# Two-layer graph network on one core: finished rows placed late, incoming rows on ScalarE, gates by row, adjacency streamed

## The chip, the cores and the metric

One core of a Trainium2 chip runs the whole kernel. A core has five engines, each with its own instruction stream that is executed in order: TensorE (PE: matmuls and transpositions), VectorE (DVE), ScalarE (ACT), GpSimd (POOL) and SyncE (SP), which here issues every DMA. [...] an instruction that waits holds up everything behind it on its engine. The metric is the device time of one launch in microseconds (us); less is better.

## The reference

Inputs: x of 16 batches, 1024 rows, 256 channels; a 1024x1024 adjacency; everything in float32.

```python
# layer 0
A_hat = (adj + I) scaled by deg**-0.5 on both sides
agg   = einsum('nm,bmd->bnd', A_hat, x)
h     = relu(batchnorm(agg @ W1.T))          # 512 wide, moments over all 16*1024 rows
y     = batchnorm(h @ W2.T)                  # 256 wide, likewise
x     = layernorm(x + y)
# layer 1, for each batch
c     = mean of x over channels              # one number per row
A     = |abs(sigmoid(c_m - c_n) - 0.5) - 0.5| * 2
g     = relu((x.T @ (adj * A)) * para)       # queries, q = g.T
k, v  = split(x @ kv_w)
attn  = softmax(q k.T * scale) over 1024 rows, 4 heads of 64
x     = layernorm(x + attn v)
```

## The kernel before

**Layer 0.** The adjacency is normalised and transposed, and aggregation and the two linear layers run over all batches, with block products arranged in a scheme of seven (`seven`). The second batch normalisation needs all rows, so its result y lies in DRAM and is normalised when it is fetched again. In this phase, `load_weights` also fetches what layer 1 keeps: `kvw`, `para_sb` and the whole adjacency `adj_sb` (32 KB of each partition).

**Layer 1** is a software pipeline over 16 batches, written out by hand. A batch has `NS` = 16 attention steps; a step is one half of the query columns (`hf`), one pair of heads and a quarter of the key rows. For a step g, `scores` makes the logits in PSUM on PE (two buffers), `exps` the exponentials on ACT (`e`, six buffers, two a step), `sums` adds them on DVE into the running denominators `acc`, and `attend` multiplies by the values on PE. All other work is cut into pieces that are placed in slots: `put(w, t, f, ...)` puts a piece into slot t of batch w. A batch has `NC` = 8 slots; slots beyond 7 belong to the next batch. Two slots make one turn, so that a batch has four turns, called 0 to 3 here. A turn issues first all pieces of its two slots and then its four attention steps. While batch b runs through attention, the slots hold:

- for batch b+1: the eight gate rows (`gate`, three in slot 0, three in slot 1, two in slot 2), keys, values (slots 0 to 2), and the query matmuls (`graph`, slots 2 to 7, with `queries` on DVE as each of four groups ends);
- for batch b+2: `load` of y and x blocks, four blocks of 256 rows (slots 0 to 3), `bn2_q` on POOL (slots 1 to 4), `rows` (transposition and residual on DVE) and `ln1_a` (statistics on DVE, inverse root on POOL) in slots 2 to 5, `ln1_b` (the normalisation itself, with a sum per row for the mean c) in slots 3 to 6, `put_x1`, `get_x1` and `x1_v` (a transposed copy by way of DRAM), `means`, and `crow` (the means as a row, broadcast by DMA);
- for batch b and the one before: `dens` (denominators by a matmul with ones, copied by ACT to `dt`), `recips`, `fetch_o` (attention output back from DRAM), `finish_a` (transposition, division, residual and statistics on DVE, scale and shift on POOL), `finish_b` (normalisation on ACT and the output DMA).

The order inside a slot is made by `arrange`: `dens` first, then `bn2_q`, then the long PE pieces (`keys`, `values`, `graph`) with the others between them by `rank`, gates ahead of them or spread among them, `recips` before the second long piece, `crow` last. In slots with `graph` the gates go first.

A gate row i is `wg_a` on ACT and, two gates later, `wg_b` on DVE. Two forms compute the same: even rows take Abs and then Tanh on ACT (lines 698, 699), odd rows a Tanh of the signed difference (line 696), whose sign bit DVE then sets with an OR (line 705). Line 706 then multiplies by the adjacency row block (128x1024).

In batch 0 there is an opening of its own (`ln1_a0`, `ln1_b0`, `gate0`, `graph0`): its rows are normalised on ACT, and PE does its query matmuls while batch 1's blocks come in. Batch 1's transposed copy is made by PE (`x1_t`). The last batch has no batch behind it.

Layer 1 assumes that no exponential overflows; it counts bad denominators, and `general`, which runs only if there are any, computes a batch again. It doesn't run with these inputs.

Of the kernel before, what the change touches and what calls it, by code (L numbers as in the profile page):

```python
# [16 lines left out]
P = 128  # L17
# [5 lines left out]
def gnn_norm_attention_kernel(  # L23
# [66 lines left out]
    c_dram = [dram.tile([NT, P], F32, name=f"crow_d{b}") for b in range(B)]  # L90
    LDP = 2
# [32 lines left out]
    with ExitStack() as l0:  # L124
# [282 lines left out]
        adj_sb = keep.tile([P, NT, N], F32, name="adj_sb")  # L407
        yts, xrs = {}, {}

        def load_weights(k):  # L410

            if k == 1:
                nc.sync.dma_start(kvw, kv_w.rearrange("(c p) f -> p c f", p=P))
            if 1 <= k <= NT // 2:
                i = 2 * (k - 1)
                nc.sync.dma_start(
                    adj_sb[:, i : i + 2, :], adj[i * P : (i + 2) * P, :].rearrange("(c p) m -> p c m", p=P)
                )
            if k == NT // 2 + 1:
                nc.sync.dma_start(para_sb, para.rearrange("o (c p) h w -> p c (o h w)", p=P))  # L420
# [139 lines left out]
    def fast():  # L560
      with ExitStack() as fx:
        pool = lambda name, bufs, **k: fx.enter_context(tc.tile_pool(name=name, bufs=bufs, **k))
        x1p = pool("x1p", 11)
# [8 lines left out]
        sm = pool("sm", 5)  # L572
        rp = pool("rp", 2)
# [40 lines left out]
        def ln1_a(b, j):  # L614
# [7 lines left out]
            mvs[b, j] = ln_stats(sm, x1s[b, j], f"a{b}_{j}")  # L622

        def ln1_b(b, j):
            mv, rs = mvs.pop((b, j))
            for a in range(2):
                r = x1s[b, j][:, a, :]
                nc.vector.scalar_tensor_tensor(
                    r,
                    r,  # L630
                    mv[:, a, 0:1],
                    rs[:, a : a + 1].to_broadcast([P, C]),
                    op0=OP.subtract,
                    op1=OP.mult,
                    accum_out=css[b][:, 2 * j + a : 2 * j + a + 1],
# [54 lines left out]

        def wg_a(b, i):
            t = wgp.tile([P, N], F32, tag="wg", name=f"wg_{b}_{i}")
            wgs[b, i] = t
            if i % 2:
# [6 lines left out]
        def wg_b(b, i):  # L701
            t = wgs[b, i]
            if i % 2:
                ti = t.bitcast(mybir.dt.int32)
                nc.vector.tensor_scalar(ti, ti, -(2**31), None, op0=OP.bitwise_or)
            nc.vector.scalar_tensor_tensor(t, t, 1.0, adj_sb[:, i, :], op0=OP.add, op1=OP.mult)  # L706
# [147 lines left out]
        def fetch_o(b, j):  # L854
# [3 lines left out]
            t = OB[b, j] = otp.tile([P, 2, C], F32, tag="ob", bufs=1, name=f"ob{b}_{j}")  # L858
# [83 lines left out]
        for b in range(B):  # L942

            for hf in range(NH):
# [3 lines left out]
                for k in range(KB // 2):  # L948
                    put(b, t + k, fetch_o, b, hf * (KB // 2) + k)
                    put(b, t + 1 + k, finish_a, b, hf * (KB // 2) + k)  # L950
                    late = 0 if b == B - 1 else 1
                    if b == B - 1 and hf == 0:
                        late = NC - t - 2 - k
                    put(b, t + 2 + k + late, finish_b, b, hf * (KB // 2) + k)
# [60 lines left out]
        def arrange(pieces):  # L1015
            first = [fa for fa in pieces if fa[0] is dens]
# [3 lines left out]
            alone = [fa for fa in pieces if fa[0] in (recips, crow)]  # L1020
# [20 lines left out]
            k = ([n for n, fa in enumerate(order) if fa[0] in long] + [len(order)] * 2)[1]  # L1041
            order[k:k] = [fa for fa in alone if fa[0] is recips]
# [4 lines left out]

        nm0 = {}

        def ln1_a0(j):  # L1050
            ln1_a(0, j)
            mv, rs = mvs.pop((0, j))
            nm = sm.tile([P, 2], F32, tag="nm", name=f"nm_a{j}")
            for a in range(2):
                nc.gpsimd.tensor_scalar(
                    nm[:, a : a + 1], mv[:, a, 0:1], rs[:, a : a + 1], -1.0, op0=OP.mult, op1=OP.mult
                )
            nm0[j] = nm, rs

        def ln1_b0(j):  # L1060
            nm, rs = nm0.pop(j)
            for a in range(2):
                r = x1s[0, j][:, a, :]
                i = 2 * j + a
                nc.scalar.activation(
                    r, r, AF.Identity, bias=nm[:, a : a + 1], scale=rs[:, a : a + 1], accum_out=css[0][:, i : i + 1]
                )
# [243 lines left out]
```

## Time and profile before

| | |
|---|---|
| time, median of 3 runs (lowest, highest) | 2517.84 us (2513.79, 2518.4) |
| the profiled execution, its time | 2517.56 us |
| its span in the profile | 2515.8 us |
| mean granted TensorE clock | 0.993 |
| from the start to the second linear layer's first stall | 610 us |
| layer 1's opening, up to the first score matmul | about 810 to 876 us |
| one batch in attention | 103.7 to 104.2 us |
| HBM traffic | 225.71 MB, 89 GB/s over the span |

The profile gives busy time by engine; groups of instructions by source line; waits, as "engine tile line <- what ended the wait: us in total, times, longest us"; and a timeline, whose columns are start, duration, engine, line, operation, output<-inputs, shapes and count, and in brackets the idle time ahead of it with what ended it. A tile's name stands without its number: `s` are the logits, `e` the exponentials, `acc` the running denominators, `pd` and `dt` the denominators, `wg` the gate rows, `pg` the query matmuls, `pk` and `pv` keys and values, `o` and `ot` the attention output, `ob` the same fetched back, `r` the finished rows, `yt` and `xr` incoming blocks, `nm` and `rs` a block's shift and scale.

### The profile page before, as it was taken

The numbers are of one execution on the slowest core, as the hardware profiler recorded it, in microseconds if no ns is written. First come the engines' busy times: TensorE is split into PE (matmuls) and PEld (weight loads), VectorE is DVE, ScalarE is ACT, GpSimd is POOL, SyncE is SP. The second block draws the span as 40 slices with busy tenths as digits, with TensorE's granted clock in tenths as the row PEclk, the third lists the DMA queues.
The fourth block names the chain that finished last, engine by engine and source line by source line (L and its number), as shares of the span: only waits on it lengthen the run. The fifth ranks groups of instructions, "written<-read, shape, count | busy, mean of one in ns | idle before, by whom it ended". The sixth has DMA issues, their size and how long they took to land.

```text
span 2515.8 us, 33531 instructions
## 1 busy us (share of the span) xinstructions
PE 2437.9 (97%) x12341; PEld 1024.0 (41%) x12341; DVE 1847.9 (73%) x2776; ACT 1037.3 (41%) x1325; POOL 694.2 (28%) x706
## 2 busy tenths in 40 slices
PE   8999999998999899999999999999999999999997
PEld 4444444443444443443434434334334343343432
DVE  5545554556767777887878879788797887978667
ACT  2000000003453355464564645636456365563644
POOL 2232322232565222222322213222132231322112
PEclk9999999999999999999999999999999999999998
DMA  3122212221796223333333333333333334333111
GB/s 134 67 84 101 99 68 84 100 97 58 265 324 201 43 55 81 68 77 80 80 76 73 77 79 77 76 79 76 80 75 74 79 73 90 71 68 89 27 42 44
DMA packets 545770, 225.71 MB, mean 90 GB/s; under 512 B 388680, under 2 KB 533696, under 8 KB 538432
## 3 DMA queue, kind: packets, MB, share of 16 engines
q1 hardware_dynamic: 545600, 223.50, 33.4%
q8 instruction: 99, 1.62, 0.3%
q14 instruction: 71, 0.58, 0.1%
HBM read 129.52 MB, written 93.91 MB: 89 GB/s over the span
## 4 chain that ended last, share of the span: by engine, by line
PE 49%; DVE 15%; ACT 7%; issue 2%; DMA 1%; SPq 0%; DVEq 0%; POOL 0%; ACTq 0%; POOLq 0%
PE pg L746 13%; PE s L772 13%; PE o L808 12%; PE po L483 7%; DVE acc L793 5%; DVE wg L706 2%; ACT wg L696 2%; ACT wg L698 1%; PE pv L732 1%; PE pd L835 1%; ACT wg L699 1%; ACT kT L724 1%; DVE st_a L551 1%; ACT e L784 1%; DVE x L607 1%
## 5 line engine op out<-in xcount | busy, mean ns | idle before, releaser
L784 ACT ACTIVATE e<-s 128x1024 f32<-128x1024 f32 x512 | 496.4, 1021 | 547.1 <-PE s L772 483.5
L793 DVE TENSOR_TENSOR acc<-acc,e 128x1024 f32<-128x1024 f32 x384 | 507.2, 1321 | 83.3 <-ACT e L784 54.0
L772 PE MATMUL s<-qT,kT 64*64 64x512 f32 x4096 | 491.8, 595 | 27.7 <-ACT e L784 26.9
L808 PE MATMUL o<-e,v 64*64 64x512 f32 x4096 | 486.1, 589 | 0.0
L746 PE MATMUL pg<-wg,x 128*128 128x512 f32 x960 | 424.9, 595 | 0.0
L603 POOL TENSOR_TENSOR yt<-yt,stq 128x512 f32<-128x512 f32 x120 | 181.3, 1511 | 446.9 <-DMA yt<-yT 185.3
L772 PEld LDWEIGHTS s<-qT,kT 64*64 64x64 f32 x4096 | 147.6, 133 | 320.2 <-issue 263.3
L808 PEld LDWEIGHTS o<-e,v 64*64 64x64 f32 x4096 | 157.0, 133 | 284.0 <-issue 271.4
L746 PEld LDWEIGHTS pg<-wg,x 128*128 128x128 f32 x960 | 178.7, 190 | 226.4 <-issue 218.7
L66 POOL TENSOR_SCALAR rs_z<-mv_z 128x2 f32<-128x2 f32 x64 | 28.2, 441 | 662.9 <-DVE mv_z L552 653.3
L102 ACT COPY u<-pa 128x512 f32<-128x512 f32 x15 | 8.8, 585 | 475.3 <-PE pa L307 475.3
L706 DVE SCALAR_TENSOR_TENSOR wg<-wg,adj_sb 128x1024 f32<-128x1024 f32 x128 | 169.7, 1345 | 14.0 <-ACT wg L699 10.6
L307 PE MATMUL pa<-AhT,x 128*128 128x512 f32 x360 | 161.8, 592 | 0.0
L721 PE MATMUL pk<-x1T,kvw 128*128 128x512 f32 x256 | 118.4, 606 | 1.3 <-DVE x1T L664 1.3
L732 PE MATMUL pv<-kvw,x1T 128*128 128x256 f32 x512 | 117.1, 382 | 0.0
L338 PE MATMUL ph<-agg,SW 128*128 128x512 f32 x240 | 112.8, 592 | 0.0
L820 DVE TENSOR_TENSOR ot<-o,ot 128x512 f32<-128x512 f32 x64 | 44.1, 689 | 93.4 <-ACT ot L819 93.4
L732 PEld LDWEIGHTS pv<-kvw,x1T 128*128 128x128 f32 x512 | 96.0, 190 | 31.5 <-issue 16.5
L307 PE MATMUL pa<-T,sx 128*128 128x512 f32 x240 | 107.9, 592 | 0.0
L307 PEld LDWEIGHTS pa<-AhT,x 128*128 128x128 f32 x360 | 68.4, 190 | 86.1 <-issue 86.1
L483 PE MATMUL po<-hL,SV 128*128 128x512 f32 x224 | 98.4, 592 | 0.0
L467 ACT ACTIVATE hL<-hL,t,s 128x512 f32<-128x512 f32 x112 | 79.7, 802 | 24.9 <-DMA hL<-h 24.9
(194 smaller groups left out, 3016.5 us busy)
## 6 DMA issues: line engine op xcount, KB each, us to landing
h<-hT SPq DMA_DIRECT2D x28, 1024.0 KB, 4.4
hL<-h SPq DMA_DIRECT2D x28, 1024.0 KB, 9.5
x<-in_x_dram SPq DMA_DIRECT2D x16, 1024.0 KB, 7.3
yT<-y SPq DMA_DIRECT2D x64, 256.0 KB, 2.6
out_dram<-r SPq DMA_DIRECT2D x64, 256.0 KB, 2.3
xr<-in_x_dram SPq DMA_DIRECT2D x62, 256.0 KB, 3.0
o<-ot SPq DMA_DIRECT2D x62, 256.0 KB, 2.3
ob<-o SPq DMA_DIRECT2D x248, 64.0 KB, 2.2
```

Source lines behind the costliest of these rows:

```text
L307: nc.tensor.matmul(p, xs[n][:, k, :], bs[n][:, k, :], start=(k == 0), stop=(k == KN - 1))
L338: nc.tensor.matmul(p, ws[n][:, ts(f, P)], bs[n], start=True, stop=True)
L483: nc.tensor.matmul(p, ws[n][:, k, :], bs[n][:, k, :], start=(k == 0), stop=(k == KF - 1))
L603: nc.gpsimd.tensor_tensor(y, y, sc, op)
L706: nc.vector.scalar_tensor_tensor(t, t, 1.0, adj_sb[:, i, :], op0=OP.add, op1=OP.mult)
L721: nc.tensor.matmul(p, kvw[:, k, ts(c, P)], x1Ts[b][:, k, ts(h, FB)], start=(k == 0), stop=(k == CT - 1))
L732: nc.tensor.matmul(p[:, ts(a, C)], x1Ts[b][:, k, ts(j + a, P)], kvw[:, k, C:], start=(k == 0), stop=(k == CT - 1),)
L746: nc.tensor.matmul(pg[b], x1s[b, k // 2][:, k % 2, ts(c, P)], wgs[b, k][:, ts(h, FB)], start=(k == 0), stop=(k == NT - 1))
L772: nc.tensor.matmul(t[r * HD : (r + 1) * HD, h, :], kTs[b, pair][h * HD : (h + 1) * HD, ts(2 * cb + r, HD)], qTs[b, pair, hf][h * HD : (h + ...
L784: nc.scalar.activation(E[g, a], S.pop((g, a)), AF.Exp)
L793: nc.vector.tensor_add(ACC[b, hf, pair], ACC[b, hf, pair], E[g, a])
L808: nc.tensor.matmul(O[b, hf, pair][r][h * HD : (h + 1) * HD, :], vs[b][r * HD : (r + 1) * HD, cb, pair * P + h * HD : pair * P + (h + 1) * HD],
```

## The change

- `finish_a` of a batch's first half of columns (`hf` 0) goes from slots 5, 6 to slots 6, 7, and that of its second half from slots 1, 2 of the next batch to slots 4, 5. `finish_b` goes from slots 7 and 0 of the next batch (first half) and 3, 4 (second half) to slots 2, 3 and 6, 7 of the next batch. So `finish_a` is in turns 2 and 3 alone, `finish_b` in turns 1 and 3. The last batch has slots of its own. `fetch_o` is issued for both blocks in the slot after the half's end, into two buffers. Buffers for `r`, statistics and `x1` grow with it.
- `ln1_b` of every batch runs on ACT, as batch 0's did; `ln1_a` gets the two POOL instructions that make its shift.
- Gate rows 0 to 4 take the signed form, rows 5 to 7 Abs and Tanh.
- The adjacency is no longer held: a ring of four row blocks of 512 KB (`adjp`), each loaded again from DRAM as soon as `wg_b` has used the block four rows before it.
- `dens` goes from the head of its slot to the place before the second long piece, `recips` to that before the third.

```diff
@@ -88,6 +88,7 @@
     st2_dram = dram.tile([2, C], F32, name="st2_d")
 
     c_dram = [dram.tile([NT, P], F32, name=f"crow_d{b}") for b in range(B)]
+    AR = 4
     LDP = 2
     s2 = const.tile([P, CT], F32, name="s2")
     t2 = const.tile([P, CT], F32, name="t2")
@@ -404,18 +405,24 @@
         nc.gpsimd.memset(ones32, 1.0)
         kvw = keep.tile([P, CT, 2 * C], F32, name="kvw")
         para_sb = keep.tile([P, CT, N], F32, name="para_sb")
-        adj_sb = keep.tile([P, NT, N], F32, name="adj_sb")
+        adjp = right("adjp", AR)
+        adjs = []
         yts, xrs = {}, {}
+
+        def load_adj():
+
+            n = len(adjs)
+            if n < B * NT:
+                t = adjp.tile([P, N], F32, tag="adj", name=f"adj{n}")
+                nc.sync.dma_start(t, adj[ts(n % NT, P), :])
+                adjs.append(t)
 
         def load_weights(k):
 
             if k == 1:
                 nc.sync.dma_start(kvw, kv_w.rearrange("(c p) f -> p c f", p=P))
-            if 1 <= k <= NT // 2:
-                i = 2 * (k - 1)
-                nc.sync.dma_start(
-                    adj_sb[:, i : i + 2, :], adj[i * P : (i + 2) * P, :].rearrange("(c p) m -> p c m", p=P)
-                )
+            if 1 <= k <= AR:
+                load_adj()
             if k == NT // 2 + 1:
                 nc.sync.dma_start(para_sb, para.rearrange("o (c p) h w -> p c (o h w)", p=P))
 
@@ -560,7 +567,7 @@
     def fast():
       with ExitStack() as fx:
         pool = lambda name, bufs, **k: fx.enter_context(tc.tile_pool(name=name, bufs=bufs, **k))
-        x1p = pool("x1p", 11)
+        x1p = pool("x1p", 12)
         x1Tp = pool("x1Tp", 1)
         crp = pool("crp", 1)
         wgp = pool("wgp", NT)
@@ -569,8 +576,8 @@
         vp = pool("vp", 2)
         ep = pool("ep", 6)
         otp = pool("otp", 3)
-        sm = pool("sm", 5)
-        rp = pool("rp", 2)
+        sm = pool("sm", 10)
+        rp = pool("rp", 4)
         ps_s = pool("ps_s", 2, space=PSUM)
         ps_t = pool("ps_t", 4, space=PSUM)
 
@@ -619,20 +626,21 @@
                         nc.tensor.transpose(p[:, a, ts(c, P)], yts[b, j][:, c, ts(a, P)], ident)
                 x1s[b, j] = x1p.tile([P, 2, C], F32, tag="x1", name=f"x1_{b}_{j}")
                 nc.vector.tensor_add(x1s[b, j], p, xrs[b, j])
-            mvs[b, j] = ln_stats(sm, x1s[b, j], f"a{b}_{j}")
+            mv, rs = ln_stats(sm, x1s[b, j], f"a{b}_{j}")
+            nm = sm.tile([P, 2], F32, tag="nm", name=f"nm_a{b}_{j}")
+            for a in range(2):
+                nc.gpsimd.tensor_scalar(
+                    nm[:, a : a + 1], mv[:, a, 0:1], rs[:, a : a + 1], -1.0, op0=OP.mult, op1=OP.mult
+                )
+            mvs[b, j] = nm, rs
 
         def ln1_b(b, j):
-            mv, rs = mvs.pop((b, j))
+            nm, rs = mvs.pop((b, j))
             for a in range(2):
                 r = x1s[b, j][:, a, :]
-                nc.vector.scalar_tensor_tensor(
-                    r,
-                    r,
-                    mv[:, a, 0:1],
-                    rs[:, a : a + 1].to_broadcast([P, C]),
-                    op0=OP.subtract,
-                    op1=OP.mult,
-                    accum_out=css[b][:, 2 * j + a : 2 * j + a + 1],
+                i = 2 * j + a
+                nc.scalar.activation(
+                    r, r, AF.Identity, bias=nm[:, a : a + 1], scale=rs[:, a : a + 1], accum_out=css[b][:, i : i + 1]
                 )
 
 
@@ -688,10 +696,12 @@
             nc.sync.dma_start(crows[b], c_dram[b].rearrange("j p -> (j p)").partition_broadcast(P))
 
 
+        SIGNED = 5
+
         def wg_a(b, i):
             t = wgp.tile([P, N], F32, tag="wg", name=f"wg_{b}_{i}")
             wgs[b, i] = t
-            if i % 2:
+            if i < SIGNED:
 
                 nc.scalar.activation(t, crows[b], AF.Tanh, bias=hcs[b][:, i : i + 1], scale=-0.5)
             else:
@@ -700,10 +710,11 @@
 
         def wg_b(b, i):
             t = wgs[b, i]
-            if i % 2:
+            if i < SIGNED:
                 ti = t.bitcast(mybir.dt.int32)
                 nc.vector.tensor_scalar(ti, ti, -(2**31), None, op0=OP.bitwise_or)
-            nc.vector.scalar_tensor_tensor(t, t, 1.0, adj_sb[:, i, :], op0=OP.add, op1=OP.mult)
+            nc.vector.scalar_tensor_tensor(t, t, 1.0, adjs[b * NT + i], op0=OP.add, op1=OP.mult)
+            load_adj()
 
         def gate(b, i):
 
@@ -855,7 +866,7 @@
             hf, k = divmod(2 * j, KB)
             if by_pe(b, hf):
                 return
-            t = OB[b, j] = otp.tile([P, 2, C], F32, tag="ob", bufs=1, name=f"ob{b}_{j}")
+            t = OB[b, j] = otp.tile([P, 2, C], F32, tag="ob", bufs=2, name=f"ob{b}_{j}")
             blk = o_dram[b, hf].rearrange("i (d e) (q n) -> q e (i d) n", e=Q, q=NQ)
             for q in range(NQ):
                 nc.sync.dma_start(
@@ -946,12 +957,14 @@
                 put(b, t, dens, b, hf)
                 put(b, t, recips, b, hf)
                 for k in range(KB // 2):
-                    put(b, t + k, fetch_o, b, hf * (KB // 2) + k)
-                    put(b, t + 1 + k, finish_a, b, hf * (KB // 2) + k)
-                    late = 0 if b == B - 1 else 1
-                    if b == B - 1 and hf == 0:
-                        late = NC - t - 2 - k
-                    put(b, t + 2 + k + late, finish_b, b, hf * (KB // 2) + k)
+                    j = hf * (KB // 2) + k
+
+                    t_a, t_b = (t + 2 + k, t + 6 + k) if hf == 0 else (t + 4 + k, t + 6 + k)
+                    if b == B - 1:
+                        t_a, t_b = (t + 2 + k, t + 3 + k) if hf == 0 else (t + 1 + k, t + 2 + k)
+                    put(b, t + 1, fetch_o, b, j)
+                    put(b, t_a, finish_a, b, j)
+                    put(b, t_b, finish_b, b, j)
             if b == 0:
                 continue
 
@@ -1013,11 +1026,11 @@
             return res + many[done:]
 
         def arrange(pieces):
-            first = [fa for fa in pieces if fa[0] is dens]
+            first = []
             gates = [fa for fa in pieces if fa[0] is gate]
             many = [fa for fa in pieces if fa[0] in long]
             first += [fa for fa in pieces if fa[0] is bn2_q]
-            alone = [fa for fa in pieces if fa[0] in (recips, crow)]
+            alone = [fa for fa in pieces if fa[0] in (dens, recips, crow)]
             few = [fa for fa in pieces if fa not in first + gates + many + alone]
             few.sort(key=lambda fa: rank.get(fa[0], len(rank)))
             few_pe = [fa for fa in few if is_short(fa)]
@@ -1038,33 +1051,14 @@
             else:
                 order = spread(order, gates)
 
-            k = ([n for n, fa in enumerate(order) if fa[0] in long] + [len(order)] * 2)[1]
-            order[k:k] = [fa for fa in alone if fa[0] is recips]
+
+            for f, k in ((dens, 1), (recips, 2)):
+                k = ([n for n, fa in enumerate(order) if fa[0] in long] + [len(order)] * 3)[k]
+                order[k:k] = [fa for fa in alone if fa[0] is f]
             return first + order + [fa for fa in alone if fa[0] is crow]
 
 
 
-
-        nm0 = {}
-
-        def ln1_a0(j):
-            ln1_a(0, j)
-            mv, rs = mvs.pop((0, j))
-            nm = sm.tile([P, 2], F32, tag="nm", name=f"nm_a{j}")
-            for a in range(2):
-                nc.gpsimd.tensor_scalar(
-                    nm[:, a : a + 1], mv[:, a, 0:1], rs[:, a : a + 1], -1.0, op0=OP.mult, op1=OP.mult
-                )
-            nm0[j] = nm, rs
-
-        def ln1_b0(j):
-            nm, rs = nm0.pop(j)
-            for a in range(2):
-                r = x1s[0, j][:, a, :]
-                i = 2 * j + a
-                nc.scalar.activation(
-                    r, r, AF.Identity, bias=nm[:, a : a + 1], scale=rs[:, a : a + 1], accum_out=css[0][:, i : i + 1]
-                )
 
         def gate0(i):
             wg_a(0, i)
@@ -1094,9 +1088,9 @@
         for j in range(NT // 2):
             bn2(0, j)
         for j in range(NT // 2):
-            ln1_a0(j)
+            ln1_a(0, j)
         for j in range(NT // 2):
-            ln1_b0(j)
+            ln1_b(0, j)
         x1_t(0, 0)
         x1_t(0, 1)
         keys(0, 0, 0)
@@ -1200,7 +1194,9 @@
             t = wg[:, i, :]
             nc.scalar.activation(t, crow, AF.Abs, bias=cs[:, i : i + 1], scale=-1.0)
             nc.scalar.activation(t, t, AF.Tanh, scale=-0.5)
-            nc.vector.scalar_tensor_tensor(t, t, 1.0, adj_sb[:, i, :], op0=OP.add, op1=OP.mult)
+            at_ = two.tile([P, N], F32, tag="adj", name=f"g_adj{i}")
+            nc.sync.dma_start(at_, adj[ts(i, P), :])
+            nc.vector.scalar_tensor_tensor(t, t, 1.0, at_, op0=OP.add, op1=OP.mult)
         kT = one.tile([P, CT, N], F32, name="g_kT")
         qT = one.tile([P, CT, N], F32, name="g_qT")
         v = one.tile([P, NT, C], F32, name="g_v")
```

## The prediction

> **What bounds it now.** I read the page's busy row first, then PE's view of waits, then the timeline of one batch by engine.
>
> ```profile
> PE 2437.9 (97%) x12341; PEld 1024.0 (41%) x12341; DVE 1847.9 (73%) x2776; ACT 1037.3 (41%) x1325; POOL 694.2 (28%) x706
> ...
> PE s L772 <- ACT e L784: 26.9, 15, 3.1
> ...
> PE pd L835 <- DVE acc L793: 4.8, 9, 1.6
> ```
>
> The tensor engine idles 78 us of 2515.8. The change alters no matmul, so it can gain only from those 78. Before 860 us lie some 38 of them (loading, the first layer, the opening chain), which it hardly touches. The view of waits (total, times, longest) shows where the rest is: 15 waits of score matmuls for an exponential, 26.9 us, and small waits of the denominator matmul for the running sum. Listing PE's gaps from the timeline: 3.12 at 894.65 (first batch), then 1.70 in each of 14 batches; seven pd waits inside the batches add to 2.70 (0.53, 0.21, 0.25, 0.28, 0.89, 0.27, 0.27), two more lie in the tail.
>
> ```profile
> 1099.02 1.90 PE L808 MATMUL o<-e,v 64*64 64x512 f32 x16
> 1102.61 2.00 PE L772 MATMUL s<-qT,kT 64*64 64x512 f32 x16 [1.70 <-ACT e L784]
> ...
> 1192.77 1.09 ACT L898 ACTIVATE r<-r,nm,rs_z 128x256 f32<-128x256 f32 x2
> 1193.77 1.14 ACT L698 ACTIVATE wg<-crow,cs 128x1024 f32<-128x1024 f32 x1
> 1194.94 1.06 ACT L699 ACTIVATE wg<-wg 128x1024 f32<-128x1024 f32 x1
> 1195.90 1.13 ACT L696 ACTIVATE wg<-crow,hcs 128x1024 f32<-128x1024 f32 x1
> ...
> 1204.15 0.59 ACT L739 COPY v<-pv 128x512 f32<-128x512 f32 x1
> 1204.62 1.16 ACT L696 ACTIVATE wg<-crow,hcs 128x1024 f32<-128x1024 f32 x1
> 1205.67 1.94 ACT L784 ACTIVATE e<-s 128x1024 f32<-128x1024 f32 x2
> ```
>
> The reader sees PE stop once per batch, in its first turn, and ACT running without a hole from the turn's start (1191.26) to the first exponential (1205.67). ACT executes in order; its queue there is six gate rows, two finished rows and copies. So the bound is PE, except in turn 0, where it is ACT. By windows a batch's turns 0 to 3 hold DVE work of 20.4, 24.6, 21.2 and 16.9 us in turns of about 25: turn 1 is DVE's full one, turn 3 its empty one.
>
> **Gate forms (sum for turn 0).** A gate by Abs and Tanh takes 1.17+0.96 = 2.13 us of ACT (starts 1193.77, 1194.94, 1195.90), the signed form 1.04. Turn 0 now has rows 0, 2, 4 as Abs (three dear, three cheap); with rows 0 to 4 signed, row 5 alone is dear: −2.18 us. finish_b leaves turn 0 (1.00 by starts). So ACT's queue is 3.2 shorter. But it can't use all of it: the copy v<-pv now waits for PE. pv ends when s starts, 1201.38; copy to 1201.9, row 5's two activations to 1203.9, first half exponential to 1204.95. The score matmul would start at 1206.75−1.70 = 1205.05. The stall should go to about 0.1. The new place of the denominators (after the first keys, not ahead of them) puts the copy dt behind gate row 1 and one keys copy; PE's reciprocal transposes come another keys piece later, so that is covered. Gain: 14×1.6 = **22.4**. In the first batch ACT starts late because the row of means arrives by DMA (1.86 wait); 2.18 of its 3.12 go: **2.2**.
> On DVE the fifth signed row costs an OR of 0.69 a batch; in turn 0 two more ORs (+1.4) stand against a finish_a of 3.4 that leaves.
>
> **finish_a and finish_b moved.** finish_a is 3.4 us of DVE (transposition 0.71, two of 0.69, statistics 1.2). It leaves turns 0 and 1; turns 2 and 3 have two each instead of one. Turn 1: 24.6 loses 3.4, one OR and 0.8 of normalising. Incoming rows, now at 1124.94, start near 1120.9, and the sums, now held up till 1132.47, can start with the first exponentials and end about 1138–1140, ahead of the pd matmul at 1140.98. Gain: the pd waits, **2.7**. Turn 2: +3.4, −1.6, and the wait of 1.98 for ob goes, its four-piece fetch being issued turns ahead (two ob buffers). Turn 3: +3.4, −0.8, into holes of 1.21, 1.06, 0.88, 0.93, 2.93: its last qT moves from 1178.4 to about 1179.8, the first exponential ends at 1179.4. Cost 0; without these holes it would be 1–2 us a batch on the sums, still a turn away from pd. finish_b: 1.0 of ACT in turns 1 and 3, in front of holes of 8–9 us.
>
> **Rows normalised on ScalarE.** 120 DVE pieces (573+82 ns by their rows) become ACT pieces of 593+187 ns (the rows of batch 0's, L1065), plus 120 POOL scalings for nm (mean 0.54 by L890's row, 0.25 when nothing runs beside). [...] Charged by piece that makes this edit a loss of 120×(0.78−0.655) = 15 us; by the timeline it is nothing, for ACT idles 8.06 us in turn 1 and 8.69 in turn 2 before the first exponential. I take nothing. But ACT now waits for POOL with the exponentials queued behind. Turn 1: rows start 1120.9, statistics done 1123.5, POOL 1.6 to 1125.1, ACT to 1126.4; the exponential is due at 1128.2, and may be 1.3 later before PE feels it. Margin 3.1.
>
> **Adjacency ring.** 124 more row loads of 512 KB less the 2 MB of the second half no longer preloaded: about +63 MB on 225.71, at DMA shares of 0.3 to 0.4. SP pays 8 issues of about 0.4 us a batch. Each waits on SP for DVE's gate product, and what stands behind it on SP waits too: ob fetches, yt loads. In turn 0 a row for gate 4 is issued about 14 us after the turn's start (two ob fetches 4, two yt loads 5, gate 1–3 in between), lands 3.7 later (the crow row's latency), and is wanted at 25: cover 7 us. Cost 0 in steady batches; without cover each late us is one on DVE, not PE.
> **In the opening it costs.** SP issued the first yt loads of batch 1 at 825.26. Now they stand behind the load of row 8, which refills row 4's buffer and so waits for gate 4's product: about 850.5. Then yt: four issues 1.9, landing 2.3, queued behind the 512 KB row (some 2): 857. POOL's two operations 2.2 each block, one block after the other (861–863 for the second), and only then, in POOL's order, the first block's rs and nm: 864.9; ACT 1.6: 866.5. PE's transposes of that block stood at 862.05. Bounds: 0, if row loads and yt overlap better, to 4.4; I take 4.2 since the chain is rowed throughout, less the two 0.37 waits for L628 that vanish: **−3.5**.
>
> **Tail.** With no batch behind it, the last has turns of some 13.8 us on PE and 12.9 on DVE with one finish_a. After: turns 0, 1 none, turns 2, 3 two each. From turn 2's start (2465.84): ot to 2467.15, finish_a 2470.5, ranges 2472, first sum 2473.4, finish_a 2476.7, six sums 7.8: 2484.5; ot, sum 2486.3, two finish_a 2493, sums 2500.8. Today they end at 2498.19 and PE waits for them. **−2.6**. Six e buffers are three steps, which just hold PE off this.
>
> **Sum.** 22.4 + 2.2 + 2.7 − 3.5 − 2.6 = 21.2 off the profiled span: 2515.8 → 2494.6. That execution took 2517.56, beside the median of 2517.84, so 2517.84 − 21.2 = **2496.6 us**.
>
> **Rivals.**
> - **The cover in opening and tail holds, or nearly** (0.12). SP's order is seen only in issue records, and yt may still land in time. Opening +0.7 and tail −1: 2517.84 − (22.4+2.2+2.7+0.7−1) = 2490.8. Against: both are chains of single engines in order.
> - **Half the stall stays** (0.18). For it: turn 0's first exponential hangs on PE's pv and one dear gate, with 0.1 to spare; crow, dt or DVE sharing with POOL (an L603 of 2 us, L706 of 1.5 instead of 1.2) could each put 1 us back. 14×0.85 lost: 2496.6+11 = 2507.6.
> - **Slower: ACT held by POOL** (0.05). ln1_b stands ahead of the exponentials in turns 1 and 2. POOL's chain of 1.5 us becomes 5.5 when DVE's sums run beside it (rs_a 1.18+1.74 at 1133.44, nm 2.54 at 1102.99), 4.0 more; a pair of L603 put in front, 4.0 more again. [...] L793 takes 1.9 us beside L603, 1.25 alone. By the free row ACT is ready 3.1 early; [...] with L603 in front 4.9 late: 14×4.9 = 69, so 2566. It decides once nm of the row block lands after 1128.2 in the batch shown. Against it: the block's statistics end before the sums start, and L603 of the next block must wait for its yt load, issued after the transposition.
> - **The ring starves DVE** (0.03): a row more than 7 us late in each batch; PE feels only what exceeds DVE's slack of 4 us. Around 2515.
> The rest, 0.62, is the forecast.
>
> **Range and chances.** Low end: opening and tail free and the stall fully gone, 2489 to 2488; high end: half the stall left and the opening at its worst, 2508. I take 2488 to 2508. No change means within 0.2%, 5 us, what this measurement can tell. Faster: forecast, first and second rival, 0.92; same 0.03, slower 0.05.
>
> **What would show it.** Right: PE's waits for e drop from 26.9 to below 4; no pd wait inside batches; L784 after gate row 5 about 1.7 earlier against s; a gap before px in the opening; pd in the tail waiting over 4 us for acc. Wrong: an ACT wait for nm with e behind it in every batch, DVE waits for the adj DMA, or period above 102.3 us (now 103.8).

## The result, and the profile after

| | before | after |
|---|---|---|
| time, median of 4 runs (lowest, highest) | 2518.07 us (2513.79, 2518.4) | 2492.94 us (2491.62, 2495.28) |
| span of the profiled execution | 2515.8 us | 2490.6 us |

The ratio of the times is 0.9905, with a 95% interval of 0.9888 to 0.9922. The forecast was 2496.6 us.

The busy row of the page of after, and the head of PE's view of waits (us in total, times, longest us):

```profile
PE 2427.3 (97%) x12341; PEld 1019.2 (41%) x12341; DVE 1798.8 (72%) x2552; ACT 1096.0 (44%) x1549; POOL 761.9 (31%) x826
```

```profile
PE s L783 <- ACT e L795: 8.7, 2, 7.8
PE px L671 <- ACT x L642: 8.2, 3, 5.8
```

The 15 waits of score matmuls are two, and the row of `pd` waiting for `acc` is gone. Between 1000 and 2280 us, twelve batches, PE's view of waits is empty. The change brought two large gaps of its own, one in the opening (5.8) and one in the last batch (7.8). The timeline shows the place where the stall was, first on PE, then on ACT:

```profile
1097.50 1.95 PE L783 MATMUL s<-qT,kT 64*64 64x512 f32 x16
1099.27 1.90 PE L819 MATMUL o<-e,v 64*64 64x512 f32 x16
1101.29 2.01 PE L783 MATMUL s<-qT,kT 64*64 64x512 f32 x16
```

```profile
1097.61 0.59 ACT L750 COPY v<-pv 128x512 f32<-128x512 f32 x1 [0.93 <-PE pv L743]
1098.09 1.15 ACT L708 ACTIVATE wg<-crow,cs 128x1024 f32<-128x1024 f32 x1
1099.27 1.06 ACT L709 ACTIVATE wg<-wg 128x1024 f32<-128x1024 f32 x1
1100.24 1.93 ACT L795 ACTIVATE e<-s 128x1024 f32<-128x1024 f32 x2
```

From `o` to the next `s` PE took 3.59 us before (1099.02 to 1102.61) and takes 2.02 now: 1.57 saved. The first exponential comes 2.74 after its scores start (4.29 before), and ACT itself now waits 0.93 for PE's `pv` on the way there.

**Where the 25.2 us of the spans come from.** The transposed means `pc` of each batch mark its start on PE; between them the two traces can be laid side by side. From the view of `pc`, before and after (first and last start in us):

```profile
L684 PE MATMUL pc<-ident,cs x15: 272/272/273, 875.5 to 2319.3; 128*8 128x128 f32 x15
```

```profile
L692 PE MATMUL pc<-ident,cs x15: 272/272/273, 881.5 to 2289.8; 128*8 128x128 f32 x15
```

| stretch | before | after | gain | predicted |
|---|---|---|---|---|
| start to batch 0's `pc` | 831.93 | 830.18 | 1.75 | 0 |
| opening, to batch 1's `pc` | 43.62 | 51.28 | −7.66 | −3.5 |
| to batch 2's `pc` (first batch) | 93.62 | 90.12 | 3.50 | 2.2 |
| 13 steady batches | 13 × 103.856 | 13 × 101.402 | 31.9 | 23.5 |
| the rest (last stall, last batch) | 196.5 | 200.79 | −4.3 | −1.0 |

The first row is no gain of the change: in the fourteen profiled executions, before and all variants, batch 0's `pc` stands between 830.0 and 833.7. The steady batches (103.46 to 104.50 before) gained 2.45 us each, more than the 1.70 and 0.2 that PE's idle time had shown there. A row that the prediction did not count, the waits of PE's weight loads, in the view of waits of before, points to the rest:

```profile
PEld pd L835 <- DVE acc L793: 27.8, 26, 2.5
```

In the timeline of before it looks like this, in two batches, turn 2:

```profile
1037.23 2.24 PE L835 MATMUL pd<-acc,ones 128*32 128x512 f32 x8
1039.41 1.13 PE L746 MATMUL pg<-wg,x 128*128 128x512 f32 x2
...
1140.98 1.05 PE L835 MATMUL pd<-acc,ones 128*32 128x512 f32 x4
1142.56 1.05 PE L835 MATMUL pd<-acc,ones 128*32 128x512 f32 x4 [0.53 <-DVE acc L793]
1143.55 1.12 PE L746 MATMUL pg<-wg,x 128*128 128x512 f32 x2
```

And after:

```profile
1140.73 1.06 PE L846 MATMUL pd<-acc,ones 128*32 128x512 f32 x8
1141.72 1.12 PE L757 MATMUL pg<-wg,x 128*128 128x512 f32 x2
```

The same eight matmuls took 2.18 us to the next group in one batch (with no idle time shown) and 2.57 in the next (0.53 shown), but 0.99 after. Over the 13 batches of before the mean is 2.28, so 1.29 a batch were lost to the sums on DVE, while the idle column showed 0.2. The reason is in the counts. After, the sums of both pairs of heads are ready, and all eight matmuls take 1.06 us: four of them start at once, and four 0.45 later. Before, only the first pair's sums are ready. Its four matmuls run alone, two at a time, and take 1.05 us, as long as all eight; the other four start when DVE has ended the second pair's. So PE counts as busy for 1.05 us of the wait, and as idle only for the rest of it. (At 1037.23 the view has drawn two such fours as one row, since the idle time between them, 0.14, is too short for it.) The sum by batch is then 1.57 + 1.29 − 0.40 = 2.46, measured 2.45. The −0.40 is the new place of `dens`, shown further down.

### The profile page after: what moved, and what is told of

Read it like the earlier page. It is cut to its first block, busy times and chain, and to the rows that moved or that the text cites. A ratio compares the mean times of both kernels' runs of the same rounds, so it can differ in the third digit from the quotient of the medians.

```text
span 2490.6 us, 33864 instructions
## 1 busy us (share of the span) xinstructions
PE 2427.3 (97%) x12341; PEld 1019.2 (41%) x12341; DVE 1798.8 (72%) x2552; ACT 1096.0 (44%) x1549; POOL 761.9 (31%) x826
## 5 line engine op out<-in xcount | busy, mean ns | idle before, releaser
L716 DVE SCALAR_TENSOR_TENSOR wg<-wg,adj 128x1024 f32<-128x1024 f32 x128 | 162.9, 1302 | 4.0 <-ACT wg L709 1.2
L66 POOL TENSOR_SCALAR rs_z<-mv_z 128x2 f32<-128x2 f32 x64 | 16.9, 265 | 482.7 <-DVE mv_z L559 401.6
L642 ACT ACTIVATE x<-x,nm_a,rs_a 128x256 f32<-128x256 f32 x128 | 75.8, 594 | 177.9 <-POOL nm_a L632 177.5
L66 POOL TENSOR_SCALAR rs_a<-mv_a 128x2 f32<-128x2 f32 x64 | 38.8, 606 | 252.9 <-DVE mv_a L559 233.5
```

The source lines that it names most:

```text
L642: nc.scalar.activation(r, r, AF.Identity, bias=nm[:, a : a + 1], scale=rs[:, a : a + 1], accum_out=css[b][:, i : i + 1])
L716: nc.vector.scalar_tensor_tensor(t, t, 1.0, adjs[b * NT + i], op0=OP.add, op1=OP.mult)
```

## The experiments

The period is the mean distance of `pc` over the 13 steady batches, which no opening or tail disturbs; the profiled execution of each run gives it. Each ratio is to before, on the same chip.

| run | what it is | median us | ratio (95%) | period | `pc` of batch 1 at |
|---|---|---|---|---|---|
| after | | 2492.94 | 0.9905 (0.9888 to 0.9922) | 101.40 | 881.5 |
| e4_gates_old | after, old gate forms | 2496.94 | 0.9915 (0.9898 to 0.9931) | 101.46 | 881.0 |
| e5_fin_old | after, old places of the finished rows | 2523.72 | 1.0019 (1.0009 to 1.003) | 104.07 | 881.9 |
| e6_fin_gates_old | after, both old | 2529.54 | 1.004 (1.0026 to 1.0055) | 103.79 | 881.7 |
| e7_ln1_dve | after, incoming rows on VectorE | 2495.54 | 0.9903 (0.9887 to 0.992) | 101.40 | 884.3 |
| e8_before_gates | before, new gate forms | 2510.45 | 0.9964 (0.9951 to 0.9976) | 103.62 | 874.4 |
| e9_fin_only | after, old gate forms, incoming rows on VectorE | 2499.71 | 0.9929 (0.9912 to 0.9946) | 101.47 | 884.4 |
| e10_before_ring | before with the ring | 2523.41 | 1.003 (1.0017 to 1.0042) | 103.65 | 884.6 |
| e11_dens_first | after, `dens` at the head of its slot | 2488.54 | 0.9877 (0.986 to 0.9893) | 101.00 | 884.7 |
| e1_tail_b | after, one `finish_b` of the last batch later | 2491.39 | 0.9898 (0.9881 to 0.9914) | 101.40 | 880.0 |
| e2_open | after, batch 1's loads ahead of the ring | 2486.1 | 0.9875 (0.9859 to 0.9892) | 101.40 | 875.5 |
| e3_both | after, e2 and the old finish slots for the last rows | 2481.14 | 0.9851 (0.9835 to 0.9868) | 101.40 | 877.3 |
| e12_best | e3 and e11 | 2475.18 | 0.9823 (0.9807 to 0.984) | 101.00 | 874.9 |

### Which part removed the stall: gate forms or finished rows?

Old gate forms in the changed kernel:

```diff
-            if i < SIGNED:
+            if i % 2:
```

> The changed kernel with the gate forms of before (even rows Abs and Tanh, odd rows signed). My step for the forms gave them 2.18 us of ACT in turn 0. Theory now: with finish_b gone from turn 0, ACT's end there is set by the copy of v behind PE and one gate row; old forms add 2.18 to ACT ahead of that copy, where it had about 1 us of waiting, and take 1.1 off behind it, so the first exponential moves by less than 0.5 us. A batch takes 101.4 to 101.8, the time is 2493 to 2499. Rival: the forms carried the gain, a batch takes 103 or more, the time 2512 or more.

The period moved by 0.05 us. All 4 us are in the first batch (94.90 instead of 90.12), where the wait for the exponential is 3.12 again. ACT in the steady turn 0, from the timeline of e4_gates_old:

```profile
1091.52 0.58 ACT L830 COPY ot<-o 128x512 f32<-128x512 f32 x1 [0.60 <-PE o L819]
...
1104.62 1.94 ACT L795 ACTIVATE e<-s 128x1024 f32<-128x1024 f32 x2
```

The exponential starts 13.10 after `ot`; with the new forms it is 13.06 (1087.18 to 1100.24), before it was 14.42 (1087.12 to 1101.54). The old forms fill ACT without a hole. The new ones are 2.18 shorter but wait 0.93 for `pv` and 1.19 for `pk`, and their one dear row stands behind `pv`. So the shorter gates gain nothing here once `finish_b` (1.0) and a wait of 0.44 for `pd` are out of ACT's queue.

Next, the old places of the finished rows for all but the last rows, alone and with the old forms:

```diff
-                    put(b, t + 1, fetch_o, b, j)
+                    t_f = t + 1
+                    if b < B - 2 or b == B - 2 and hf == 0:
+                        t_f, t_a, t_b = t + k, t + 1 + k, t + 3 + k
+                    put(b, t_f, fetch_o, b, j)
```

> The changed kernel with fetch_o, finish_a and finish_b of batches 0 to 13 and of batch 14's first half back in their old slots; forms, ln1_b on ACT, ring and dens as changed. Theory: ACT waits about 2 us in turn 0 of the changed kernel (0.28, 0.80, 0.93), so finish_b's 1.0 fits there and the score stall stays gone; DVE's turn 1 has 3.4 more, but lost an OR and a normalisation (1.5), and ends its sums about when dens asks. A batch takes 101.4 to 101.9, the time is 2493 to 2500. Rival: moving the finished rows carried the gain; a batch takes 102.5 or more, the time 2508 or more.

> As e5_fin_old, and with the old gate forms as well. Theory: each of the two edits alone empties ACT's turn 0 enough, and only both undone bring the stall back: e4's ACT is full from gate row 2 to the exponentials, so finish_b's 1.0 comes on top. PE waits about 1 to 1.2 for e in each batch's turn 0, a batch takes 102.4 to 103.6, the time is 2510 to 2526. Rival (the stall left by another edit, such as the place of dens): as e4, below 2500.

Both are slower than the kernel before. In e5 the theory failed: turn 0 has no wait for an exponential, as it said, but a new stall stands in turn 1. In e6, a little slower than expected, the stall of turn 0 is back in another place: PE waits 0.96 there in each batch for `dt`, the copy of the denominators, which ACT makes late, and 0.87 in turn 1 for an exponential. ACT in turn 1, from the timeline of e5_fin_old:

```profile
1131.01 0.60 ACT L642 ACTIVATE x<-x,nm_a,rs_a 128x256 f32<-128x256 f32 x1 [9.69 <-POOL nm_a L632]
...
1132.19 1.91 ACT L795 ACTIVATE e<-s 128x1024 f32<-128x1024 f32 x2
```

PE at the same place:

```profile
1133.24 2.00 PE L783 MATMUL s<-qT,kT 64*64 64x512 f32 x16 [1.69 <-ACT e L795]
```

And ACT after:

```profile
1124.06 0.60 ACT L642 ACTIVATE x<-x,nm_a,rs_a 128x256 f32<-128x256 f32 x1 [3.87 <-POOL nm_a L632]
...
1126.93 1.94 ACT L795 ACTIVATE e<-s 128x1024 f32<-128x1024 f32 x2 [1.60 <-PE s L783]
```

The batch of e5 started 2.0 us later. With `finish_a` in turn 1, DVE takes the incoming rows only at 1126.75 (1119.55 after), their shift `nm_a` comes at about 1131, and ACT, which executes in order, holds the exponentials behind the waiting row: PE waits 1.69 in the batch shown. Without `finish_a` there is time: ACT is done with the rows at 1125.34 and then waits for PE. This is the effect of the prediction's slower rival, ACT held with the exponentials behind it, but not by its cause: POOL's chain is no slower than after (about 1.6 us, from 1129.54); it starts late, because DVE's statistics end only at 1129.38. In the changed kernel the moved rows keep it out of the steady batches.

The mirror image, the kernel before with the new gate forms alone:

```diff
-            if i % 2:
+            if i < 5:
```

> The kernel before with the new gate forms (rows 0 to 4 signed) and nothing else. Theory: 2.18 us less of ACT in turn 0 end most of the 1.9 us that PE lost there, and 2 to 4 in the first batch; the pd waits of turn 2 stay (about 1.2 a batch by start to start), opening and tail lose nothing. A batch takes 102.1 to 102.5, the time is 2492 to 2499, as good as the whole change. Rival: the two more ORs in DVE's turn 0 (1.4) lengthen the pd waits; a batch takes 103 or more.

This missed: 2510.45 us. The stall of turn 0 does go, so for that either part suffices; but the head of PE's waits in e8_before_gates is now

```profile
PE pd L835 <- DVE acc L793: 21.3, 15, 2.8
```

and the timeline shows turn 2's denominators held longer than before:

```profile
1133.78 1.05 PE L835 MATMUL pd<-acc,ones 128*32 128x512 f32 x4
1136.48 1.05 PE L835 MATMUL pd<-acc,ones 128*32 128x512 f32 x4 [1.65 <-DVE acc L793]
1137.46 1.12 PE L746 MATMUL pg<-wg,x 128*128 128x512 f32 x2
```

3.68 us to the next group, where the batch of before that is shown above has 2.57; over the 13 batches 3.55 against 2.28. So of the 1.57 that turn 0 gave, 1.28 went into this wait, and the batch gained 0.24. From the first gate product of turn 0 to the last sum of turn 1, DVE has two holes only in the batch shown (0.92 and 0.38), and its sums end just 0.4 earlier than before, counted from `pc`. DVE was a second bound just behind the first. The number is also that of the run's rival: the new forms put two more ORs into DVE's turn 0 and take one out of turn 1. What they add to the wait was not separated.

Last, the changed kernel with old gate forms and with `ln1_b` on VectorE again, so that the moved rows, the ring and the places of `dens` and `recips` remain:

> The changed kernel with the old gate forms and with ln1_b of batches 1 to 15 on DVE, so that of the work that moves only the finished rows are placed anew (ring and dens as changed). Theory: finish_a's two times 3.4 us out of DVE's turns 0 and 1 and finish_b's 1.0 out of ACT's turn 0 carry the whole gain of a batch: 101.4 to 101.7 a batch, 2496 to 2501 in all (the forms' 4 us in the first batch are missing). Rival: it takes all three to make room; a batch takes 102.5 or more, the time over 2508.

Its period is 101.47: of the parts in question, the places of the finished rows alone make the steady gain. (The ring and the place of `dens` stay in; their own effects, −0.2 and +0.4, follow below.)

### Incoming rows on ScalarE

```diff
+            if b > 0:
+                mvs[b, j] = mv, rs
+                return
...
+                if b == 0:
...
+                    continue
+                nc.vector.scalar_tensor_tensor(
+                    r,
+                    r,
+                    nm[:, a, 0:1],
+                    rs[:, a : a + 1].to_broadcast([P, C]),
+                    op0=OP.subtract,
+                    op1=OP.mult,
+                    accum_out=css[b][:, i : i + 1],
```

> The changed kernel with ln1_b of batches 1 to 15 on DVE as before, in its slots. Theory: DVE's turn 1 has 2 to 3 us of room since finish_a left it, so 0.8 to 0.9 us a block cost nothing: 101.4 to 101.6 a batch, time within 3 us of 2493. Rival: ScalarE's share of the work is what ends the pd waits; a batch takes 102 or more, the time over 2500.

The period is the same to 0.01 us, so in the batches nothing pays for the longer pieces on ACT, and nothing is gained by them. The run is 2.6 us longer in the median; the intervals of the two ratios overlap. In the opening there may be a gain: from `pc` to `pc` it takes 53.3 to 54.0 us in the three runs that have these rows on VectorE under the ring (e7, e9, e10), and 49.5 to 51.7 in the six with them on ScalarE and with the opening as in after (after, e1, e4, e5, e6, e11). No run was made to test this.

### The ring: opening and steady batches

The ring alone, on the kernel before, with the same `load_adj` after each gate product as in the change:

```diff
-        adj_sb = keep.tile([P, NT, N], F32, name="adj_sb")
+        adjp = right("adjp", AR)
...
-            nc.vector.scalar_tensor_tensor(t, t, 1.0, adj_sb[:, i, :], op0=OP.add, op1=OP.mult)
+            nc.vector.scalar_tensor_tensor(t, t, 1.0, adjs[b * NT + i], op0=OP.add, op1=OP.mult)
+            load_adj()
```

> The kernel before with the adjacency in the ring of four, nothing else. Theory: in steady batches the ring is free (103.7 to 103.9 a batch), and it alone makes the opening late, by SP's order: first yt issues near 849, PE waits 5 to 7 us before px, the time is 2522 to 2528. Rival: its 63 MB slow the other transfers, and a batch takes over 104.3; or the opening's loss came with ln1_b on ACT, and the time is 2518.

The period did not suffer (103.65 against 103.86), so a row block is there in time. Batch 1's `pc` stands 9.0 us later than before (10.4 counted from batch 0's `pc`), and PE waits 8.38 ahead of `px`, more than the 5 to 7 expected. The rows are on VectorE here, so the loss did not come with ScalarE. The timeline of after shows how, on PE and then on SP (SP's rows are issues):

```profile
866.30 1.27 PE L671 MATMUL px<-ident,x 128*128 128x128 f32 x4 [5.84 <-ACT x L642]
867.37 6.07 PE L1074 MATMUL pg<-wg,x 128*128 128x512 f32 x8
```

```profile
835.16 14.01 SPq L417 DMA_DIRECT2D adj<-in_adj_dram  x5
849.28 1.96 SPq L443 DMA_DIRECT2D yt<-yT  x4
```

SP waits for DVE's gate products with batch 1's first blocks behind it, and PE runs dry. The refills also fill the DMA engines: their share is 1.01 between 857 and 866 (0.58 before), and the second block's `yt` is with POOL only 5.2 us after its last issue (2.7 before). Then it is slow as well: 6.07 us for eight matmuls that take 3.60 elsewhere. The windows of after (stretch, length, PE busy and its matmuls, granted clock, DMA share, GB/s):

```profile
866.00:870.00 4.00, 3.70 (x8) 0.50 0.58 123
870.00:875.00 5.00, 5.00 (x13) 0.77 0.00 0
```

The fix issues the two blocks ahead of the ring, which takes them out of both queues at once:

```diff
-                put(b - 2, j, load, b, j)
+                if b > 1 or j >= LDP:
+                    put(b - 2, j, load, b, j)
...
         for j in range(NT // 2):
             ln1_b(0, j)
+        for j in range(LDP):
+            load(1, j)
```

> The changed kernel with the first two loads of batch 1 issued ahead of gate row 0, so that they don't stand on SP behind the adjacency loads; nothing else. Theory: SP's order costs the opening. First yt issues near 825 instead of 849, PE's wait of 5.84 us before px falls below 1, the half clock after it doesn't occur, the transposition of the means of batch 1 stands near 874 instead of 881.5, and the time falls by about 7.5 to 2485.4. Rival: normalising on ACT by way of POOL makes the chain late; then a wait of 3 us or more for x stays and the gain is under 3 us.

PE's timeline in e2_open:

```profile
862.72 0.60 PE L671 MATMUL px<-ident,x 128*128 128x128 f32 x4
863.15 3.60 PE L1075 MATMUL pg<-wg,x 128*128 128x512 f32 x8
```

No gap, a granted clock of 1.00 from 862 to 870, and 6.8 us less than after in the medians (6.2 in the spans).

### The tail

The last batch's `finish_b` of its first block, one slot later:

```diff
-                        t_a, t_b = (t + 2 + k, t + 3 + k) if hf == 0 else (t + 1 + k, t + 2 + k)
+                        t_a, t_b = (t + 2 + k, NC) if hf == 0 else (t + 1 + k, t + 2 + k)
```

> The changed kernel with finish_b(15,0) moved from slot 127 (the turn in which its finish_a runs) to slot 128; nothing else. Theory: in the last turn ACT waited 6.38 us at line 909 for POOL's shift of r, with the exponentials queued behind, so PE stood 7.82 us and then ran at half clock for some 1.6 us more. Then PE's wait for e in the last turn falls below 1 us, what is left is DVE's late sums as predicted (pd waits 2 to 3 us), and the time falls by about 3 from 2492.9 to 2490. Rival: DVE is so late by itself that the e buffers are full; then PE still waits over 4 us for e there, and the time stays within 1 us of 2492.9.

After, ACT and then PE in the last batch:

```profile
2460.88 1.33 ACT L909 ACTIVATE r<-r,nm,rs_z 128x256 f32<-128x256 f32 x2 [6.38 <-POOL nm L901]
```

```profile
2463.16 3.51 PE L783 MATMUL s<-qT,kT 64*64 64x512 f32 x16 [7.82 <-ACT e L795]
```

The change puts this `finish_b` into the same turn as its own `finish_a`. ACT reaches it before POOL has the shift, and the exponentials stand behind it. POOL is not slow here either: it starts at 2459.43, right after DVE's statistics (2459.27). In e1_tail_b that wait is gone, and PE waits where the prediction had it:

```profile
2468.86 1.92 PE L846 MATMUL pd<-acc,ones 128*32 128x512 f32 x4 [5.55 <-DVE acc L804]
```

That wait is longer than the 2 to 3 us expected. The stretch from the last `pc` to the end falls by 1.4 us only (200.8 to 199.4), and the medians by 1.5, which this measurement can't tell from nothing; the other 2.0 of the 3.4 us by which the span falls lie ahead of it, where nothing was changed.

e3_both has the fix of the opening and gives the last batch, and the second half of the one before it, their old finish slots:

```diff
-                    put(b, t + 1, fetch_o, b, j)
+                    t_f = t + 1
+                    if b == B - 1 or b == B - 2 and hf == 1:
+                        t_f, t_a = t + k, t + 1 + k
+                        t_b = t + 3 + k if b == B - 2 else NC if hf == 0 else t + 2 + k
+                    put(b, t_f, fetch_o, b, j)
```

> The changed kernel with the loads of the opening as in e2_open and with the last two batches' fetch_o, finish_a and finish_b in the slots that they had before the change. If opening and tail are the only places where the change lost, the gains add: 7.5 from the opening and 5.5 from the tail, 2480 us, and one batch still takes 101.4. If the tail's old order loses by something else, 2484 or more.

2481.14 us: the tail is 196.4 us again, as before the change (196.5), and the opening is about as short as in e2_open (43.7 us from `pc` to `pc`, against 42.9 there and 51.3 after). The old tail was not run without the new opening.

### The place of the denominators, and all repairs together

```diff
-            first = []
+            first = [fa for fa in pieces if fa[0] is dens]
...
-            alone = [fa for fa in pieces if fa[0] in (dens, recips, crow)]
+            alone = [fa for fa in pieces if fa[0] in (recips, crow)]
...
-            for f, k in ((dens, 1), (recips, 2)):
...
+            k = ([n for n, fa in enumerate(order) if fa[0] in long] + [len(order)] * 2)[1]
+            order[k:k] = [fa for fa in alone if fa[0] is recips]
```

> The changed kernel with dens and recips in their old places of a slot. Theory: in the changed kernel DVE ends its sums of turn 1 about 2.3 us ahead of the turn's end, so pd needs no cover any more: no pd wait in the batches, a batch 101.2 to 101.4, the time within 2 us of 2493. Rival: the new place hides waits of pd; they come back at 0.5 us or more a batch, the time is 2500 or more.

It came out better than that: 0.40 us less in every batch. Turn 0 on PE, first after and then e11_dens_first:

```profile
1087.08 1.98 PE L732 MATMUL pk<-x1T,kvw 128*128 128x512 f32 x4
...
1095.68 1.89 PE L743 MATMUL pv<-kvw,x1T 128*128 128x256 f32 x8
```

```profile
1089.10 1.07 PE L846 MATMUL pd<-acc,ones 128*32 128x512 f32 x8
...
1097.50 1.89 PE L743 MATMUL pv<-kvw,x1T 128*128 128x256 f32 x8
```

With `dens` behind the first keys, the keys, denominators and reciprocals of turn 0 take 8.60 us (1087.08 to 1095.68); with `dens` at the head the same matmuls take 8.40 (1089.10 to 1097.50). In turn 2 it is 10.42 against 10.21. They are cut into one more piece, and each cut cost 0.20. PE shows no wait in either, since `acc` is ready by now. Why a cut costs this much was not looked into.

> The changed kernel with three repairs: batch 1's first blocks loaded ahead of the adjacency rows, the last two batches' finished rows in their old slots, and the denominators again at the head of their slot. If the three repairs are independent, the time is that of the run with the first two, 2481.1, less the 0.40 us a batch that the old place of the denominators gave alone: 14 x 0.4 = 5.6, so 2475 to 2477, with a period of 101.0 us and at most 2.5 us of waiting for exponentials. The rival: with the tail's old slots the denominators at the head of the slot bring PE's waits for acc forward in the last batch (the tail of the run with the old place alone was 201.2 against 200.8), and 2480 or more is measured.

2475.18 us, a ratio of 0.9823 (0.9807 to 0.984) to before; inside the 2475 to 2477 that independent repairs give. PE's waits for exponentials and for `acc` in e12_best:

```profile
PE pd L846 <- DVE acc L804: 2.4, 1, 2.4
...
PE s L783 <- ACT e L795: 1.7, 2, 1.1
```

## Why the prediction was right, and where it was not

The time was 3.7 us under the forecast and inside the range. That it came so near is in part luck, for the small error is a sum of larger ones of both signs: +8.4 in the steady batches, −4.2 in the opening, +1.3 in the first batch, −3.3 in the tail and +1.75 ahead of batch 0's `pc`, together +4.0 on the spans.

- **The stall of turn 0** (14 × 1.6 = 22.4): right in size. It measured 1.57, so 14 × 1.57 = 22.0. The step named "Gate forms" put the causes together wrongly, though. It charged 2.18 to the forms and 1.0 to `finish_b` and already saw that the copy of `v` waits for PE. It did not draw the conclusion that either alone removes the stall: e4 (forms taken back) loses 0.05 a batch, e8 (forms alone) has no such stall but loses the gain to DVE, and e6 (neither) has it back.
- **The pd waits** (2.7): the mis-sized term. They were 13 × 1.29 = 16.8. The prediction added up PE's idle column, which leaves out the time in which four matmuls run alone (1.05 us, as against 1.06 for all eight); the distance between starts holds it. That DVE's turn 1 loses `finish_a` and that the sums then run with the exponentials was right: they end at 1137.4 (predicted 1138 to 1140), before `pd` at 1140.73.
- **Rows on ScalarE** (0, against 15 by piece): right, by e7. The wait for POOL with the exponentials behind it was seen, and so was its point of decision, 1128.2. After, ACT starts the rows at 1124.06 and passes; e5, at about 1131 (1129 on the clock of after's batch), stalls.
- **Ring, steady batches** (0): right, by e10. **Opening** (−3.5): the cause was right, but it cost 7.7. That `px` stands at 866.30 (predicted 866.5) is luck: this execution runs 1.75 earlier up to batch 0's `pc`, and counted from there `px` is 6.0 late instead of 4.2. The first block was with POOL as forecast, but the second came 6.9 us behind it (854.85 to 861.75) where the step had 4: ahead of its `yt` stand two refills and an issue of `xr` that took 1.90 instead of 0.43, and the DMA engines were full (a share of 1.01 from 857 to 866). Then the clock after the gap (0.50 from 866 to 870), which the step left out, makes the way from `px` to `pc` 1.66 longer (15.16 instead of 13.50). The loads of SP stood in the trace of before; that PE slows after such a gap did too, after the gap of 3.12 at 894.65 (0.57 from 895 to 899).
- **Place of `dens`** ("covered"): it is covered on ACT, but the switch on PE costs 0.40 a batch, 13 × 0.40 = 5.2.
- **First batch** (2.2): 3.5. The wait fell from 3.12 to 0.84, as the step had it (2.28), and the slow matmuls after the longer gap (sixteen of `s` in 3.30 us, 2.00 after) went with it.
- **Tail** (−2.6): DVE's sums end 35.2 after turn 2's start in e1, as predicted (35.0). But the step left out that `finish_b` stands one slot behind its `finish_a` there, so that ACT is held as in the slower rival (6.38 us), in the last batch alone. From `pd` of its turn 0 (2435.86 and 2405.20) to the end it took 79.94 before and 85.4 after, −5.5.
- **Signs that were named**: no `pd` wait inside batches, the gap before `px`, and a period under 102.3 came, and the exponential behind gate row 5 is 1.55 earlier against `s` (about 1.7 named). Waits for `e` below 4 did not (8.7, of which 7.8 is the tail), and `pd` in the tail did not wait for `acc`, because PE was already late.
- **Rivals**: the first had opening and tail nearly free; they lost 7.7 and 5.5. The second (half the stall stays) had `crow`, `dt` or DVE putting 1 us back; 0.3 is left. The third, ACT held by a slow POOL, did not come in the steady batches; POOL's chain for the rows of turn 1 took 1.6 us (1122.64 to 1124.26). That rival's 4.9 us were the author's estimate from rows of before: 4.0 + 4.0, less the margin of 3.1. In the trace of after such a chain takes 5.3 us, for the next block beside the sums on DVE (1132.20 to 1137.48); why was not shown. The ring starved nothing.

## What to carry to other kernels

When a wait is to be removed, look for the second-latest engine behind it, and measure what it costs by the distance between starts of the waiting engine's groups, not by its idle column (1.29 us a batch against 0.2 here): it says what the first repair is worth alone (0.24 of 1.57 us in e8). A piece that waits for another engine, put into an in-order queue ahead of the critical work, was free here or cost whole microseconds depending on one arrival time (no wait of PE in the steady batches of after, 1.69 us in e5, 7.82 in the last batch of after); look at it again in the first and in the last round, where the cover is missing. And when a preloaded tensor becomes a ring, its refills may stand in the queue ahead of the loads that the opening needs (7.7 us lost here), so issue these first (6.8 us less in e2_open).

## What the hardware showed that was not expected

- **Four narrow matmuls took as long as eight.** Of the denominators' matmuls (weights 32 columns wide, one strip of the output each), four started at once when all sums were ready (1140.73 of after), and eight took 1.06 us; when only one pair's sums were ready (1140.98 of before), two started at once, and four took 1.05.
- **A gap cost twice.** After PE's 5.84 us gap the granted clock is 0.50 over the next 4 us and 0.77 over the 5 after that; after the 7.82 us gap it is 0.58 over 4 us, and sixteen matmuls take 3.51 us instead of 1.90. After before's gap of 3.12 it is 0.57 from 895 to 899. After a gap of 1.70 it is 1.00 (1102 to 1106 of before).
- **An issue took longer on SP than elsewhere.** With 512 KB rows queued (a DMA share of 1.12 from 851 to 853.3 and 1.04 from 856.6 to 860), the issues of `xr` at 851.29 and 856.65 of after took 1.90 and 3.23 us; the same issue takes 0.43 in e2_open at 828.97, ahead of the rows.
